# A message-passing kernel: 23 slots of 128 edges whose node features VectorE copies column by column in SBUF, in place of POOL's gathers

## The chip, the core and the metric

The kernel runs on one core of a Trainium2 chip. Its engines are PE (TensorE, matrix products), DVE (VectorE), ACT (ScalarE), POOL (GpSimd) and SP (SyncE, which only issues transfers here); each runs its own queue of instructions in order, and semaphores tie them together. SBUF is the on-chip memory, PSUM holds what PE writes. The metric is the device time of one execution in microseconds (us), the median of several runs; one more execution is taken with the hardware profiler.

## The reference

A graph has 12,500 nodes with 64 features (`x`) and 200,000 edges, sorted by their target `dst`. For each edge the features of its source and its target node go through a small network, the 64 edge features through another, and the product of both, scaled by a cutoff of the distance, is added up at the target node:

```python
nodes = node_state[edges].reshape(num_edges, -1)          # x[src], x[dst]
gates = ssp(edge_state @ We1 + be1) @ We2 + be2
gates = gates * (1.0 - sigmoid(5.0 * (edges_distance - (CUTOFF - 1.5))))
h = ssp(nodes @ Wn1 + bn1) @ Wn2 + bn2
message_sum = zeros_like(node_state).at[edges[:, 1]].add(h * gates)
new_state = node_state + (ssp(message_sum @ Ws1 + bs1) @ Ws2 + bs2)
return layernorm(x + new_state)
```

`ssp` is softplus less log 2. All is float32.

## The kernel before

**Steps and slots.** The edges are worked off in `NG` = 391 steps of 512 edges. A step has K = 4 slots of 128 edges, one edge to a partition. `src` is random, so the source features of a slot are fetched row by row; `dst` is sorted, so the targets of 256 edges lie within a window of 42 nodes, and the kernel reads that window's part of a table (x times the lower half of Wn1, made in the preparation) as a piece of a weight matrix `wns`.

**How the source rows come in.** For most slots POOL issues one indirect transfer each (`gather`, L231), which fetches 128 rows of 64 values into `xg[:, k, :64]`; tile `xg` has AHEAD + BEHIND = 19 buffers, and the program asks for step i + 14 in step i. A gather has to wait until its buffer's old tile is no longer read, that is, for the scatter product of the step 19 earlier. 47 of the 1,564 slots (`slots_by_rows`) are instead fetched by 128 single-row transfers, 7 in each step from SP's queue and 9 from ACT's (`fetch`, L257), and DVE copies the comparison's columns next to them (L296).

**One step i of the main loop**, in the order in which it is written; every engine takes its part in that order (`manual_schedule`):

- SP: loads for step i + 5 (edge features `eT`, L278; table pieces into `wns`, L286), then 7 row fetches. POOL: the gathers of step i + 14.
- PE: four transposes of step i + 1 (`tx`, L307), which turn edges x features into features x edges. ACT copies the result to SBUF (`xT`, L314).
- PE: bias products (L319, L354); the scatter product of step i - 2 (L383), which adds up messages by the comparison's ones and zeros; the edge product (L324); the node product `wns` x `xT` (L330), two halves h of 256 edges, of slots k = h and k = 2 + h. ACT takes exponential and logarithm of the result (L341, L344).
- DVE: `window` adds the scatter product to `sums` at two positions that are known only at run time (L400; the positions are loaded into DVE's registers by L391). PE: second layer of step i (L361 and L366, from `s`). DVE: two products with the cutoff (`hcut` L375, `message` L379), then softplus of step i + 1 (L349, writes `s`), then `onehot` of step i + 3: a comparison of the edges' targets with 0 to 41 (L293, writes `xg[:, :, 64:106]`).
- Parts of finished blocks of 512 nodes (`node_block`) are spread over the steps, some before `onehot`, some behind it.

**Preparation.** 56 gathers are issued at the start. PE makes the table in 14 pieces (L591), ACT and DVE copy each to SBUF (L593, L594, tile `tb`), SP stores it (L595), and DVE clears `sums` behind it (L596). In between, behind the fourth piece, DVE prepares positions and biases (L598 to L605), and behind the sixth `rel` (L609, L612).

**Registers.** A position known at run time is read from SBUF by the engine's own sequencer (`values_load_multi_w_load_instructions`, a TENSOR_LOAD in the trace), and a FUSED_REGOPS works out the address ahead of each instruction that uses it.

Of the kernel before, what the change touches and what calls it, by code (L numbers as in the profile page):

```python
# [42 lines left out]
F32 = mybir.dt.float32  # L43
# [35 lines left out]
READY = (5, 7)  # L79
LANDED = 4  # L80
CUTOFF = 5.0
EPS = 1e-5
# [22 lines left out]
def slots_by_rows(NG):  # L105

    slots = []
    for queue in range(2):
        n = 0
        for g in range(READY[queue], NG - 2):  # L110
            if (g - READY[queue] - ROWS_FROM + 1) * ROWS[queue] >= (n + 1) * P:
                slots.append((queue, g, K - 1 - queue))
                n += 1
    return slots


# [7 lines left out]
def gnn_resnorm_kernel(ctx: ExitStack, tc: tile.TileContext, a: dict, out: bass.AP, E: int):  # L124
# [58 lines left out]
    row3 = const.tile([PIECES, 2, K, D], BF16, name="row3")  # L183
    rs3 = const.tile([PIECES, K, D], BF16, name="rs3")
    wns = const.tile([DW, REST, 2, 2 * D], F32, name="wns")

# [34 lines left out]
    def gather(g):  # L221
# [3 lines left out]
        for k in range(K):  # L225
            if (g, k) in by_rows:
                continue
            if padding(g, k):
                nc.vector.memset(xg[:, k, :D], 0.0)
                continue  # L230
            note(("gather", g), nc.gpsimd.indirect_dma_start(  # L231
                out=xg[:, k, :D], out_offset=None, in_=x,
                in_offset=bass.IndirectOffsetOnAxis(ap=src_i[:, g, k : k + 1], axis=0)))
# [39 lines left out]
    def load(g):  # L273
# [11 lines left out]
        for h in range(2):  # L285
            behind(note(("load", g), nc.sync.dma_start(  # L286
                wns[D:DW, g % REST, h, :].bitcast(U8),
                table_bytes[:, bass.ds(bases[g][h], 8 * D * W)].rearrange("o (w f) -> (o w) f", w=W))), old)

    xTs, zs, us, ss, ghs, hs, msgs, scs = ({} for _ in range(8))  # L290

# [35 lines left out]
    def layer1_node(g):  # L327
        for h in range(2):
            zn = zs[g][:, h, HE * (1 - h) : HE * (2 - h)]
            nc.tensor.matmul(zn, wns[:, g % REST, h, :], xTs[g][:, h], start=True, stop=True,  # L330
                             skip_group_check=True)

    def z_of(g):
# [156 lines left out]
    with tc.manual_schedule():  # L490
# [4 lines left out]
        with tc.tile_pool(name="prep", bufs=1) as prep:  # L495
# [11 lines left out]
            for i in range(3):  # L507
                load_x(i)
            nc.sync.dma_start(rows_i, a["rows"])
            dist = cut.rearrange("p g k -> p (g k)")  # L510
            nc.sync.dma_start(dist, a["dist_l"])
# [3 lines left out]
            for g in range(AHEAD):  # L515
# [13 lines left out]
            nc.scalar.dma_start(wns[:D].rearrange("f r h o -> f (r h) o"),  # L529
                                a["Wn1"][:D, :].rearrange("f (r o) -> f r o", r=1).to_broadcast([D, 2 * REST, 2 * D]))  # L530

            dst_f = dst_h.bitcast(F32)
# [53 lines left out]
            for i in range(PARTS):  # L586
# [10 lines left out]
                if i == 1:  # L597
                    nc.vector.tensor_copy(base_i[:1], base_b[:1])  # L598
                    nc.vector.tensor_scalar(base_i[32:33], base_b[32:33], float(8 * D), None, OP.mult)
                    nc.vector.tensor_scalar(rows_i, rows_i, float(4 * D), None, OP.mult)  # L600
                    for k in range(2):
                        nc.vector.tensor_copy(be3[:, k, :], rows[:, 0, :])
# [11 lines left out]

        with tc.tile_pool(name="finish", bufs=1) as finish:
            blocks = list(zip(node_blocks(N), block_steps(N, NG)))
            last = NG - 1
# [14 lines left out]
            for i in range(-1, last - 1):  # L632
                now = parts.pop(i, [])
                early = [part for part in now if part.tensor]
                at(load, i + LOADS)
                read_rows(i, 0, ROWS[0])
                fetch(i, 0, ROWS[0])
# [24 lines left out]
                for part in early:  # L662
                    part.others()
                at(onehot, i + 3)
                for part in now:
                    if not part.tensor:
# [133 lines left out]
def layouts(inputs):  # L800
# [22 lines left out]
    for queue, columns in enumerate(row_columns(NG)):  # L823
        chosen = [out["src_l"].reshape(P, NG, K)[:, g, k] for q, g, k in slots_by_rows(NG) if q == queue]
        v = padded(np.concatenate(chosen), P * columns, 0).reshape(-1, P, READ)
        rows.append(v.transpose(1, 0, 2).reshape(P, columns))
    out["rows"] = np.ascontiguousarray(np.concatenate(rows, axis=1))
    out["dst_l"] = lanes(dst, dst[-1])
    out["dist_l"] = lanes(dist, 1e6)
# [43 lines left out]
```

## Time and profile before

| | |
|---|---|
| runs | 2685.64 us median of 3 (2685.46 to 2688.31) |
| profiled execution | 2686.47 us; span 2684.7 us |
| granted TensorE clock | 0.815 on average |
| busy | PE 84%, PEld 65%, POOL 54%, DVE 39%, ACT 36% |
| gathers (L231) | 1,516, 951 ns each |
| DMA | 53 GB/s on average |

The profile is of one execution. In a line of the timeline the first number is the start in us from the span's start, the second the time it took; what stands in brackets is the idle time of the engine just before it and what ended that. In a group's line the numbers behind the count are the busy time, the mean of one in ns, and the idle time before the group's instructions with what ended most of it. PE and PEld are the products and the weight loads of TensorE; the ends of products are modelled. A releaser is inferred from semaphores, and "remote" and "issue" are what is left where none was found.

### The profile page before, as it was taken

The page shows a single profiled execution, that of the slowest core. Times are in us where ns is not written, and L with a number is a line of the kernel's source. Part 1 is how long each engine was busy: PE and PEld are TensorE (multiplying, and loading weights), DVE is VectorE, ACT ScalarE, POOL GpSimd, SP SyncE. Part 2 cuts the span into 40 slices and gives each one's busy share as a digit, 9 for nine tenths or more (in the row PEclk, how much of TensorE's full clock was granted, in tenths as well). Part 3 has the DMA queues.
Part 4 walks back from the last instruction along what each step waited for, and adds up shares of the span by engine and source line. Part 5 has one row for each costly group of instructions (what it writes and reads, how often), then busy time and mean ns, then how long its engine had stood idle before and what let it go on. Part 6 is the DMA issues. An engine that isn't in the chain of part 4 may idle for free.

```text
span 2684.7 us, 47845 instructions
## 1 busy us (share of the span) xinstructions
PE 2243.6 (84%) x11373; PEld 1754.9 (65%) x11373; DVE 1052.4 (39%) x2767; ACT 969.6 (36%) x1318; POOL 1441.8 (54%) x1520
## 2 busy tenths in 40 slices
PE   2489888988888888888889788888888888888897
PEld 1467666766666666666667666666666667666676
DVE  1233333333334333344333443434433443444445
ACT  0133333333333333333333333333334333333344
POOL 7335555555555555555555555555555555555520
PEclk9987788788788778788777888778878887787878
DMA  6222222222222212222222222222222222222210
GB/s 159 82 64 52 48 51 49 48 49 48 49 52 50 49 47 51 51 52 47 52 46 50 51 49 53 53 50 53 51 50 50 50 58 48 54 52 50 52 44 25
DMA packets 150911, 143.53 MB, mean 53 GB/s; under 512 B 51887, under 2 KB 98395, under 8 KB 150626
## 3 DMA queue, kind: packets, MB, share of 16 engines
q1 hardware_dynamic: 94090, 88.26, 11.6%
q0 software_dynamic: 48512, 49.77, 9.5%
q10 hardware_dynamic: 8024, 2.37, 0.4%
q8 instruction: 97, 1.59, 0.2%
q14 instruction: 188, 1.54, 0.2%
HBM read 130.59 MB, written 9.63 MB: 52 GB/s over the span
## 4 chain that ended last, share of the span: by engine, by line
PE 64%; another core or an unknown queue 11%; ACTq 10%; ACT 7%; issue 5%; DVE 1%; DMA 0%; DVEq 0%; SPq 0%
PE z L330 16%; PE gh L366 12%; PE z L383 10%; ACTq L257 10%; PE gh L361 7%; PE tx L307 6%; ACT xT L314 6%; PE z L324 4%; PE gh L354 3%; PE z L319 2%; PE tx L419 1%; PE z L591 1%; ACTq L245 1%; PE tx L450 1%
## 5 line engine op out<-in xcount | busy, mean ns | idle before, releaser
L231 POOL DMA_INDIRECT xg<-in_x,src_i x1516 | 1441.6, 951 | 1144.8 <-PE z L383 353.1
L330 PE MATMUL z<-xT,wns 106*128 106x256 f32 x1564 | 574.1, 503 | 322.9 <-ACT xT L314 309.5
L330 PEld LDWEIGHTS z<-xT,wns 106*128 106x128 f32 x1564 | 361.3, 246 | 486.6 <-ACT xT L314 407.9
L341 ACT ACTIVATE u<-z 128x768 f32<-128x768 f32 x392 | 317.4, 810 | 830.4 <-issue 362.4
L366 PE MATMUL gh<-consts,s 128*128 128x64 f32 x3128 | 493.1, 313 | 0.0
L400 DVE TENSOR_TENSOR sums<-sums,z 64x42 f32 x778 | 153.0, 197 | 863.4 <-issue 626.8
L366 PEld LDWEIGHTS gh<-consts,s 128*128 128x128 f32 x3128 | 490.2, 238 | 0.1
L314 ACT COPY xT<-tx 106x512 f32<-106x512 f32 x391 | 228.9, 586 | 670.9 <-remote 231.5
L375 DVE TENSOR_TENSOR h<-gh,cut 128x256 f32<-128x256 f32 x391 | 166.1, 425 | 618.2 <-PE z L383 239.7
L344 ACT ACTIVATE u<-u,one 128x768 f32<-128x768 f32 x392 | 365.9, 934 | 69.7 <-issue 53.3
L349 DVE SCALAR_TENSOR_TENSOR s<-u,z 128x768 f32<-128x768 f32 x392 | 369.4, 943 | 11.1 <-ACT u L344 9.8
L361 PEld LDWEIGHTS gh<-consts,s 128*128 128x128 f32 x1564 | 304.0, 247 | 70.1 <-DVE s L349 32.8
L383 PEld LDWEIGHTS z<-xg,msg 128*128 128x128 f32 x1556 | 240.3, 221 | 152.8 <-issue 148.5
L361 PE MATMUL gh<-consts,s 128*128 128x128 f32 x1564 | 313.8, 335 | 1.8 <-DVE s L349 1.8
L383 PE MATMUL z<-xg,msg 128*128 128x84 f32 x1556 | 306.2, 327 | 0.9 <-DVE msg L379 0.2
L324 PE MATMUL z<-eT,consts 128*128 128x256 f32 x782 | 295.4, 465 | 0.0
L307 PE MATMUL tx<-consts,xg 128*106 128x128 f32 x1517 | 278.6, 312 | 6.4 <-DMA wns<-table 6.4
L307 PEld LDWEIGHTS tx<-consts,xg 128*106 128x106 f32 x1517 | 216.0, 169 | 10.6 <-issue 8.0
L379 DVE TENSOR_TENSOR msg<-gh,h 128x256 f32<-128x256 f32 x391 | 166.0, 425 | 13.4
L354 PE MATMUL gh<-row,ones 3*128 3x512 bf16 x391 | 170.0, 435 | 0.0
L324 PEld LDWEIGHTS z<-eT,consts 128*128 128x128 f32 x782 | 141.7, 226 | 1.2 <-issue 1.2
L293 DVE TENSOR_TENSOR xg<-consts,rel 128x168 f32<-128x168 f32 x391 | 129.9, 332 | 0.0
(93 smaller groups left out, 609.5 us busy)
## 6 DMA issues: line engine op xcount, KB each, us to landing
xr<-in_x ACTq DMA_DIRECT2D x3328, 0.2 KB
eT<-in_eT SPq DMA_DIRECT2D x195, 256.0 KB
xr<-in_x SPq DMA_DIRECT2D x2688, 0.2 KB
xg<-in_x,src_i POOLq DMA_INDIRECT x1516
wns<-table SPq DMA_DIRECT2D x782, 21.0 KB
table<-tb SPq DMA_DIRECT2D x14, 448.0 KB
sums<-in_xT SPq DMA_DIRECT2D x7, 455.0 KB
y<-in_x SPq DMA_DIRECT2D x24, 128.0 KB
```

The costliest lines, as they stand in the source:

```text
L231: note(("gather", g), nc.gpsimd.indirect_dma_start(out=xg[:, k, :D], out_offset=None, in_=x, in_offset=bass.IndirectOffsetOnAxis(ap=src_i[ ...
L257: ins = queues[queue].dma_start(row_tiles[n, "in"][r : r + 1, :D].bitcast(U8), x_bytes[:, bass.ds(row_at[queue].pop(0), 4 * D)])
L307: ins = nc.tensor.transpose(tx[:, k, :], xgs[g][:, k, :DW], ident)
L314: note(("xcopy", g), nc.scalar.copy(xT, xTs[g]))
L324: nc.tensor.matmul(zs[g][:, 0, :HE], we1.rearrange("a h d -> a (h d)"), eTs[g], start=False, stop=True, skip_group_check=True)
L330: nc.tensor.matmul(zn, wns[:, g % REST, h, :], xTs[g][:, h], start=True, stop=True, skip_group_check=True)
L341: nc.scalar.activation(us[g][:, part], z_of(g)[:, part], AF.Exp)
L344: nc.scalar.activation(us[g][:, part], us[g][:, part], AF.Ln, bias=one)
L349: nc.vector.scalar_tensor_tensor(ss[g].rearrange("p i t e -> p (i t e)")[:, part], us[g][:, part], BIG, z_of(g)[:, part], OP.min, OP.max)
L361: nc.tensor.matmul(v[:, 0, t], ss[g][:, 0, t, :], we2, start=False, stop=False, skip_group_check=True)
L366: nc.tensor.matmul(ghs[g][:, 1, 2 * t + h, :], ss[g][:, 1 + h, t, :], wn2, start=False, stop=h == 1 and t == 1, skip_group_check=True)
L383: ins = nc.tensor.matmul(sc, msgs[g][:, 2 * t : 2 * t + 2, :].rearrange("p h f -> p (h f)"), xgs[g][:, 2 * t : 2 * t + 2, D:DW], start=t = ...
```

## The change

For 23 slots (k = 1 of steps 26, 42, ... 378; `slots_by_columns`), POOL no longer gathers. A transposed copy `xh` of x lies in SBUF: 128 partitions x 6,250, nodes 0 to 6,249 in the upper 64 partitions and nodes 6,250 to 12,499 in the lower 64. From step 8 on DVE, behind `onehot`, loads eight column numbers into registers and copies eight columns of `xh`, one for each of eight edges, into a tile `column` of 128 x 128; after 16 steps the tile is full. One DVE instruction then keeps, for each edge, the half of the partitions that holds its node (`sides` against `border`) and writes `chosen`. In the step's node product PE adds `wn1_twice` x `chosen` for that slot. In `xg` the slot's 64 columns are set to zero by DVE, so the transposes and the product with `wns` stay as they were and add only the target's part. `xh` is loaded in four parts from SP's queue in steps 0 to 3; column numbers, sides and the doubled weights are loaded and converted in the preparation.

```diff
@@ -78,6 +78,9 @@
 ROWS_FROM = -1
 READY = (5, 7)
 LANDED = 4
+COLUMNS = 8
+COLUMNS_FROM = 8
+XH_PARTS = 4
 CUTOFF = 5.0
 EPS = 1e-5
 LN2 = 0.6931471805599453
@@ -112,6 +115,20 @@
                 slots.append((queue, g, K - 1 - queue))
                 n += 1
     return slots
+
+
+def slots_by_columns(NG):
+
+    slots = []
+    for g in range(NG - 2):
+        if (g - 3 - COLUMNS_FROM + 1) * COLUMNS >= (len(slots) + 1) * P:
+            slots.append((g, 1))
+    return slots
+
+
+def column_columns(NG):
+
+    return -(-len(slots_by_columns(NG)) // COLUMNS) * COLUMNS
 
 
 def row_columns(NG):
@@ -182,6 +199,14 @@
     be3 = const.tile([PIECES, 2, D], BF16, name="be3")
     row3 = const.tile([PIECES, 2, K, D], BF16, name="row3")
     rs3 = const.tile([PIECES, K, D], BF16, name="rs3")
+    half_n = a["xh"].shape[1]
+    by_columns = {slot: n for n, slot in enumerate(slots_by_columns(NG))}
+    columns_i = const.tile([P, column_columns(NG)], I32, name="columns_i")
+    sides_i = const.tile([P, len(by_columns) * P], I32, name="sides_i")
+    sides = sides_i.bitcast(F32)
+    sign = const.tile([P, 1], F32, name="sign")
+    border = const.tile([P, 1], F32, name="border")
+    wn1_twice = const.tile([P, 2 * D], F32, name="wn1_twice")
     wns = const.tile([DW, REST, 2, 2 * D], F32, name="wns")
 
     xgs, xrs, eTs = {}, {}, {}
@@ -225,7 +250,7 @@
         for k in range(K):
             if (g, k) in by_rows:
                 continue
-            if padding(g, k):
+            if padding(g, k) or (g, k) in by_columns:
                 nc.vector.memset(xg[:, k, :D], 0.0)
                 continue
             note(("gather", g), nc.gpsimd.indirect_dma_start(
@@ -287,6 +312,28 @@
                 wns[D:DW, g % REST, h, :].bitcast(U8),
                 table_bytes[:, bass.ds(bases[g][h], 8 * D * W)].rearrange("o (w f) -> (o w) f", w=W))), old)
 
+    column_tiles, chosen_columns, columns_done = {}, {}, [0]
+
+    def columns(i, pool):
+
+        n = columns_done[0]
+        if i < COLUMNS_FROM or n >= len(by_columns) * P:
+            return
+        p, q = (n // COLUMNS) % P, n // (COLUMNS * P) * COLUMNS
+        _, at = nc.values_load_multi_w_load_instructions(
+            columns_i[p : p + 1, q : q + COLUMNS], engines=[DVE], min_val=0, max_val=half_n - 1,
+            skip_runtime_bounds_check_because="src holds rows of x")
+        slot = list(by_columns)[n // P]
+        if n % P == 0:
+            column_tiles[slot] = pool.tile([P, P], F32, name="column", bufs=1)
+        for j in range(COLUMNS):
+            nc.vector.tensor_copy(column_tiles[slot][:, n % P + j : n % P + j + 1], xh[:, bass.ds(at[j], 1)])
+        columns_done[0] += COLUMNS
+        if columns_done[0] % P == 0:
+            chosen_columns[slot] = pool.tile([P, P], F32, name="chosen", bufs=1)
+            nc.vector.scalar_tensor_tensor(chosen_columns[slot], sides[:, n // P * P : (n // P + 1) * P], border,
+                                           column_tiles[slot], OP.is_ge, OP.mult)
+
     xTs, zs, us, ss, ghs, hs, msgs, scs = ({} for _ in range(8))
 
     def onehot(g):
@@ -327,8 +374,12 @@
     def layer1_node(g):
         for h in range(2):
             zn = zs[g][:, h, HE * (1 - h) : HE * (2 - h)]
-            nc.tensor.matmul(zn, wns[:, g % REST, h, :], xTs[g][:, h], start=True, stop=True,
+            chosen = [t for t in range(2) if (g, 2 * t + h) in by_columns]
+            nc.tensor.matmul(zn, wns[:, g % REST, h, :], xTs[g][:, h], start=True, stop=not chosen,
                              skip_group_check=True)
+            for t in chosen:
+                nc.tensor.matmul(zn[:, t * P : (t + 1) * P], wn1_twice, chosen_columns[g, 2 * t + h], start=False,
+                                 stop=True, skip_group_check=True)
 
     def z_of(g):
         return zs[g].rearrange("p b e -> p (b e)")[:, : 3 * HE]
@@ -507,6 +558,8 @@
             for i in range(3):
                 load_x(i)
             nc.sync.dma_start(rows_i, a["rows"])
+            nc.sync.dma_start(columns_i, a["columns"])
+            nc.sync.dma_start(sides_i, a["sides"].partition_broadcast(P))
             dist = cut.rearrange("p g k -> p (g k)")
             nc.sync.dma_start(dist, a["dist_l"])
             dst_i = rel.bitcast(I32)
@@ -528,6 +581,11 @@
             nc.scalar.dma_start(consts[:, FIRST:], a["consts"][:, FIRST:])
             nc.scalar.dma_start(wns[:D].rearrange("f r h o -> f (r h) o"),
                                 a["Wn1"][:D, :].rearrange("f (r o) -> f r o", r=1).to_broadcast([D, 2 * REST, 2 * D]))
+
+            for h in range(2):
+                nc.scalar.dma_start(wn1_twice[h * D : (h + 1) * D, :], a["Wn1"][:D, :])
+                nc.vector.memset(sign[h * D : (h + 1) * D], 2.0 * h - 1.0)
+                nc.vector.memset(border[h * D : (h + 1) * D], float(half_n if h else 1 - half_n))
 
             dst_f = dst_h.bitcast(F32)
             nc.vector.tensor_copy(dst_f, dst_h)
@@ -598,6 +656,10 @@
                     nc.vector.tensor_copy(base_i[:1], base_b[:1])
                     nc.vector.tensor_scalar(base_i[32:33], base_b[32:33], float(8 * D), None, OP.mult)
                     nc.vector.tensor_scalar(rows_i, rows_i, float(4 * D), None, OP.mult)
+                    upper = prep.tile([P, column_columns(NG)], F32, name="upper")
+                    nc.vector.tensor_scalar(upper, columns_i, float(half_n), float(-half_n), OP.is_ge, OP.mult)
+                    nc.vector.tensor_tensor(columns_i, columns_i, upper, OP.add)
+                    nc.vector.tensor_scalar(sides, sides_i, sign, None, OP.mult)
                     for k in range(2):
                         nc.vector.tensor_copy(be3[:, k, :], rows[:, 0, :])
                     for k in range(K):
@@ -613,6 +675,7 @@
 
 
         with tc.tile_pool(name="finish", bufs=1) as finish:
+            xh = finish.tile([P, half_n], F32, name="xh")
             blocks = list(zip(node_blocks(N), block_steps(N, NG)))
             last = NG - 1
             parts, begun, complete, rest = {}, None, 0, []
@@ -633,6 +696,9 @@
                 now = parts.pop(i, [])
                 early = [part for part in now if part.tensor]
                 at(load, i + LOADS)
+                if 0 <= i < XH_PARTS:
+                    part = slice(half_n * i // XH_PARTS, half_n * (i + 1) // XH_PARTS)
+                    nc.sync.dma_start(xh[:, part], a["xh"][:, part])
                 read_rows(i, 0, ROWS[0])
                 fetch(i, 0, ROWS[0])
                 if i >= 0:
@@ -662,6 +728,7 @@
                 for part in early:
                     part.others()
                 at(onehot, i + 3)
+                columns(i, finish)
                 for part in now:
                     if not part.tensor:
                         part.others()
@@ -825,6 +892,12 @@
         v = padded(np.concatenate(chosen), P * columns, 0).reshape(-1, P, READ)
         rows.append(v.transpose(1, 0, 2).reshape(P, columns))
     out["rows"] = np.ascontiguousarray(np.concatenate(rows, axis=1))
+    chosen = np.concatenate([out["src_l"].reshape(P, NG, K)[:, g, k] for g, k in slots_by_columns(NG)])
+    out["sides"] = np.ascontiguousarray(chosen)
+    v = padded(chosen, P * column_columns(NG), 0).reshape(-1, P, COLUMNS)
+    out["columns"] = np.ascontiguousarray(v.transpose(1, 0, 2).reshape(P, -1))
+    half_n = -(-N // 2)
+    out["xh"] = np.ascontiguousarray(np.concatenate([x[:half_n].T, padded(x[half_n:], half_n, 0.0).T]))
     out["dst_l"] = lanes(dst, dst[-1])
     out["dist_l"] = lanes(dist, 1e6)
     out["dst_h"] = np.ascontiguousarray(padded(dst, NR * P * HE, dst[-1]).reshape(NR, P, HE).transpose(1, 0, 2))
```

## The prediction

> **What bounds the kernel now.** First the page: busy shares and the costliest groups.
>
> ```profile
> PE 2243.6 (84%) x11373; PEld 1754.9 (65%) x11373; DVE 1052.4 (39%) x2767; ACT 969.6 (36%) x1318; POOL 1441.8 (54%) x1520
> ...
> L231 POOL DMA_INDIRECT xg<-in_x,src_i x1516 | 1441.6, 951 | 1144.8 <-PE z L383 353.1 <-issue 352.1 <-DVE s L349 182.5
> ```
>
> PE looks like the bound, POOL like an engine with half its time free. So I asked next for the busy time in two stretches of 71 us: one in which POOL has no gathers left, and one in the middle.
>
> ```profile
> 2589.00:2660.00 71.00, 68.98 (x446) 56.93 (x446) 42.61 (x118) 36.60 (x55) 0.00 (x0) 0.97 0.11 31
> 1480.00:1551.00 71.00, 58.58 (x309) 46.20 (x309) 28.25 (x76) 27.15 (x38) 40.22 (x44) 0.83 0.22 52
> ```
>
> The columns are PE, PEld, DVE, ACT and POOL busy, granted clock, DMA share, GB/s. Without gathers PE is 97% busy at a clock of 0.97, and a step (from one xT copy, L314, to the next) takes 4.58 us on average over the last 14. With them PE is 83% busy. What PE waits for stands in the timeline of POOL and that of ACT, around a step that issues three gathers:
>
> ```profile
> 1553.31 0.95 POOL L231 DMA_INDIRECT xg<-in_x,src_i  x1 [1.50 <-DVE s L349]
> 1554.56 0.95 POOL L231 DMA_INDIRECT xg<-in_x,src_i  x1 [0.30 <-issue]
> 1555.82 0.95 POOL L231 DMA_INDIRECT xg<-in_x,src_i  x1 [0.30 <-issue]
> 1558.25 0.94 POOL L231 DMA_INDIRECT xg<-in_x,src_i  x1 [1.48 <-PE z L383]
> 1559.49 0.95 POOL L231 DMA_INDIRECT xg<-in_x,src_i  x1 [0.30 <-issue]
> 1560.75 0.95 POOL L231 DMA_INDIRECT xg<-in_x,src_i  x1 [0.30 <-issue]
> 1562.00 0.95 POOL L231 DMA_INDIRECT xg<-in_x,src_i  x1 [0.30 <-issue]
> ```
>
> ```profile
> 1553.00 0.59 ACT L314 COPY xT<-tx 106x512 f32<-106x512 f32 x1 [1.65 <-PE z L383]
> ...
> 1557.94 0.59 ACT L314 COPY xT<-tx 106x512 f32<-106x512 f32 x1 [0.94 <-PE z L383]
> ...
> 1564.27 0.59 ACT L314 COPY xT<-tx 106x512 f32<-106x512 f32 x1 [2.37 <-remote]
> ```
>
> The xT copy starts 2.12 us after the start of the last gather of its batch (1555.82 to 1557.94), and again 2.27 us after (1562.00 to 1564.27); 0.31 us later POOL starts the next batch, which waits for the scatter of the same step (a tile has 19 buffers, and POOL has used them all). Over steps 20 to 369 that distance is 1.9 to 2.6 us in 92% of them, while the distance from the end of the transposes, for which the copy waits, runs from 0.04 to 3 us. So PE's finished work is told to the others only when the batch of gathers is through; why, the trace does not show. A step is then three issue intervals of 1.25 us, 2.2 us and 0.31 us: 6.26 us, and with one gather fewer 5.01. Medians: 6.37 for 302 steps with four, 5.12 for 41 with three.
>
> **Part by part.** Base: the profiled execution took 2686.47 us (span 2684.7 and 1.8 around it), 0.83 above the median of 2685.64.
>
> *Removed: 23 gathers.* They are 16 steps apart (g = 26, 42, ... 378). The 41 steps with three gathers price one, since the kernel already fetches 47 slots in another way. Not all of 1.25 us stays: after such a step PE may be late. A step with three and the next, which has four, take 12.55 us together, two with four 13.29: 0.74 saved. Over three steps it is 18.84 against 19.99 (1.15, standard error 0.22), over five 32.16 against 33.39 (1.24, 0.20). I take 1.0: 23 x 1.0 = -23 us; ends 0.74 and 1.25, -17 and -29. POOL's queue loses only these; the zeroing of xg's 64 columns instead is a DVE memset (L229: 112 ns), whose waits are for gathers of 19 tiles ago.
>
> *Added on DVE in 368 steps:* one load of eight registers and eight copies, each with a register operation. The load is like L391's (median 528 ns; it runs in DVE's queue, ahead of the engine). A copy of 128x1 is not in the trace: small copies follow each other by 0.09 to 0.10 us (L602 to L605, 110.03 to 110.87), the two dynamic additions of `window` by 0.20, held to the end of the first. So eight take 0.8 to 1.6 us. What is queued behind them is the next `window`, whose own load (0.53) and register operation (0.09) no longer run early: 1.42 us at least, 2.8 if the first load is bare too. The cover:
>
> ```profile
> 1506.42 0.94 DVE L349 SCALAR_TENSOR_TENSOR s<-u,z 128x768 f32<-128x768 f32 x1
> 1507.28 0.33 DVE L293 TENSOR_TENSOR xg<-consts,rel 128x168 f32<-128x168 f32 x1
> 1510.04 0.41 DVE L400 TENSOR_TENSOR sums<-sums,z 64x42 f32 x2 [2.43 <-issue]
> 1510.50 0.42 DVE L375 TENSOR_TENSOR h<-gh,cut 128x256 f32<-128x256 f32 x1
> ```
>
> The copies go between L293 and L400, an idle stretch of 2.23 us on average. Then L375 waits another 1.64 for PE, and from the end of L349 to L361, which reads s, there are 1.50. Taking these three from 1.42 and from 2.8 us step by step, L375 is late by 6.6 and 61 us in sum, L361 by 0 and 7. PE is reached last, so: +1 us, ends 0 and 7.
>
> *Added on PE:* 23 matmuls of 128x128 f32 in `layer1_node`; transposes and the old product stay. L361 has the shape: 335 ns a record, two records, 0.11 us apart at full clock, so 0.22 to 0.27 us: 6 us if all count. In 85% of steps PE's work is over 0.3 us or more ahead of its signal, and that cover hides them: +2, ends 0 and 6. The 23 selections (128x128, two inputs, like L569's 272 ns) go into the same DVE idle stretch.
>
> *Preparation.* DVE multiplies `sides`, 128x2944, int32 to f32. L609 (128x1564) took 0.90 us, so about 1.7; with two small ones (L600: 0.19 each) 2.1. At L612's rate (0.97 us for 782) it would be 4. They sit between the fourth and fifth copy to `tb` (107.28 and 110.95), and PE's run L591 x112 from 111.55 to 135.84, without a gap, starts on the fifth: +2.1, on the path. The three small transfers and the 1.5 MB broadcast of `sides` are issued early on SP's and ACT's queues, ahead of dist, dst and four parts of xT on SP's; all of these are wanted after 106 us, behind the stream of 56 gathers (to 99.5 us). If they slow that stream, 0 to 2: +0.5. The four parts of `xh` (0.8 MB each) go out in steps 0 to 3 on SP's queue, behind loads for five steps later and ahead of the row fetches of the step; the stores to the table showed 448 KB every 3 us, so each part takes up to 5.4 us beside gathers. Signals 1 us late in four steps give +4: I take +1.
>
> Sum: -23 + 1 + 2 + 2.1 + 0.5 + 1 = -16.4, so 2686.5 - 16.4 = 2670.
>
> **A rule against the change.** Does a copy from SBUF to SBUF hold a gather? Row: a gather that starts while a copy runs,
>
> ```profile
> 2181.45 0.95 POOL L231 DMA_INDIRECT xg<-in_x,src_i  x1 [3.11 <-PE z L383]
> 2181.45 0.22 DVE L296 COPY xr<-xg 128x42 f32<-128x42 f32 x1
> ```
>
> and one that starts 0.04 us behind the start of L293, an operation with two inputs in SBUF:
>
> ```profile
> 353.47 1.11 POOL L231 DMA_INDIRECT xg<-in_x,src_i  x1 [2.69 <-PE z L383]
> ```
>
> The five gathers with L296 running at their start took 946 ns each, those just behind L293 up to 1.11 us. So I set the copies at nothing. The Trainium skill (SBUF — State Buffer, Who interferes with whom) says otherwise: an fp32 copy within SBUF can run in a two-port mode that takes the port pair shared with GpSimd, and the later of the two blocks until the other ends. By it eight copies of 0.1 us would hold POOL 0.8 us in each of 368 steps, of which 85% count: +250 us, 2920. The trace's copies are wider than one element and only 47, so it does not settle the case fully.
>
> **Rivals.** (1) *The copies hold the gathers:* slower. For it: L293 does it, and copies now run at the first and second gather of nearly every step. Against it: the rows above. Price: 0.155 us (1.107 less 0.952) on one gather a step, x 368 x 0.85 = 48 us, so 2718; half of it 2694. It decides from 16.4 / (368 x 0.85) = 0.05 us a step, a mean gather above about 965 ns. (2) *PE takes the gain back:* the clock is granted at 0.8 between 0.5 and 1.0, and steps just behind a three-gather step are often over 7 us. At 0.3 us a gather, -7 + 6.6 = 0: 2686. (3) *DVE is late:* 3.8 us instead of 1.42 to 2.8 puts L361 30 us late in sum: 2699.
>
> **Chances.** Forecast 0.62 (2657 to 2681; of that 0.02 within 0.2%), rival 2 0.14 (same 0.10, faster 0.02, slower 0.02), rivals 1 and 3 together 0.24 (slower 0.23, same 0.01). 0.2%, 5.4 us, is about what a measurement of this kernel can tell from no change. That gives faster 0.64, same 0.13, slower 0.23. The unknowns reach from 2686.5 - 29 + 2 = 2660 to 2686.5 - 17 + 23 = 2692; taking in half of rivals 1 and 3 on top and a little below: 2656 to 2700.
>
> **What would show it.** Right: 1493 gathers with a mean near 951 ns; xT copies still 2.2 us behind the last gather; 23 more steps near 5.1 us; POOL still idle about 1.5 us a step; L400's wait shorter, L361's waits for s still small; PE's long L591 run from about 114. Wrong: gathers above 965 ns on average (rival 1), step sums around the new short steps not shorter (rival 2), PE waiting for s by tens of us (rival 3).

## The result, and the profile after

Over 20 runs of each kernel the changed one takes 2694.31 us (median) and the one before 2682.32: a ratio of 1.0048, 95% interval 1.0027 to 1.0069. The change makes this kernel slower, by 12 us where 16 less were forecast. The profiled execution took 2700.15 us (span 2698.2, granted clock 0.807; before 2686.47, 2684.7, 0.815).

In the page after, the busy shares and four groups answer to those shown of before (line numbers are those of the changed kernel: gather L256, `hcut` L426, `window` L451, column copies L330):

```profile
PE 2275.5 (84%) x11419; PEld 1778.3 (66%) x11419; DVE 1283.1 (48%) x5764; ACT 969.1 (36%) x1318; POOL 1415.2 (52%) x1497
...
L256 POOL DMA_INDIRECT xg<-in_x,src_i x1493 | 1415.0, 948 | 1188.0 <-PE z L434 387.4
...
L426 DVE TENSOR_TENSOR h<-gh,cut 128x256 f32<-128x256 f32 x391 | 165.8, 424 | 760.3 <-PE tx L354 242.1
...
L451 DVE TENSOR_TENSOR sums<-sums,z 64x42 f32 x778 | 152.9, 197 | 470.6 <-issue 330.8
...
L330 DVE COPY column<-xh 128x1 f32 x2944 | 244.2, 144 | 35.4 <-issue 34.6
```

The 23 gathers are gone, and the others are no longer than they were (948 ns, before 951), so the copies do not hold POOL. POOL waits for PE's scatter product longer nevertheless (387.4 us, before 353.1). DVE's wait ahead of `window` is shorter, as was meant (470.6, before 863.4 at its L400), but its wait ahead of `hcut`, for PE, is 142 us longer (760.3, before 618.2 at its L375). In the stretches of 71 us, the middle of the kernel and the end without gathers:

```profile
1480.00:1551.00 71.00, 63.80 (x314) 48.99 (x314) 35.33 (x162) 26.77 (x38) 39.27 (x42) 0.78 0.21 51
2600.00:2671.00 71.00, 66.44 (x430) 54.99 (x429) 45.33 (x144) 36.76 (x55) 2.66 (x3) 0.98 0.13 37
```

At the end, where all but three gathers are through, little has changed: clock 0.98, and the last 14 steps take 4.60 us on average (before 4.58). In the middle PE works off about as many products (314, before 309) in more busy time, at a clock of 0.78. The loss lies in the steps that gather: steps 20 to 369 take 6.562 us on average, before 6.531, although 59 of them have fewer than four gathers, before 44. A step with four takes 6.772 us (before 6.679).

What has grown is the last piece of a step, from the start of the batch's last gather to the next xT copy; I call it the *tail*. The prediction took it as fixed at 2.2 us. Over steps 20 to 369 of the two traces it takes 2.31 us on average, before 2.20, which is 39 us in sum. (The way from an xT copy to the first gather takes 8 us more in sum, that from the first gather to the last 37 less.) PE being late is not what makes most of it. In the steps in which the transposes, for which the xT copy waits, had ended over 0.3 us before it (by their modelled ends), the tail is 2.25 us (305 steps), before 2.15 (297), which makes some 29 of the 39 us. I call these steps *held*.

A second thing is new in the timeline of DVE, set against ACT's xT copy. Before the change:

```profile
1510.04 0.41 DVE L400 TENSOR_TENSOR sums<-sums,z 64x42 f32 x2 [2.43 <-issue]
1510.50 0.42 DVE L375 TENSOR_TENSOR h<-gh,cut 128x256 f32<-128x256 f32 x1
1510.95 0.42 DVE L379 TENSOR_TENSOR msg<-gh,h 128x256 f32<-128x256 f32 x1
1511.42 0.95 DVE L349 SCALAR_TENSOR_TENSOR s<-u,z 128x768 f32<-128x768 f32 x1
```

```profile
1513.60 0.59 ACT L314 COPY xT<-tx 106x512 f32<-106x512 f32 x1 [2.21 <-PE z L383]
```

`hcut` starts 3.1 us ahead of the next xT copy, and the softplus that PE needs for its next second layer is ready 1.2 us ahead of it. After the change:

```profile
1512.63 0.42 DVE L426 TENSOR_TENSOR h<-gh,cut 128x256 f32<-128x256 f32 x1 [2.31 <-PE z L434]
1513.09 0.42 DVE L430 TENSOR_TENSOR msg<-gh,h 128x256 f32<-128x256 f32 x1
1513.43 0.94 DVE L400 SCALAR_TENSOR_TENSOR s<-u,z 128x768 f32<-128x768 f32 x1
```

```profile
1512.74 0.59 ACT L361 COPY xT<-tx 106x512 f32<-106x512 f32 x1 [1.73 <-remote]
```

Here `hcut` waits until the moment in which the xT copy too is released, behind the batch of gathers, and softplus is ready only 1.6 us into the next step. The prediction knew that the xT copy is told of PE's work only when the batch is through. It had not seen that the second layer's signal was told in the middle of the batch in 57% of these 350 steps before the change (`hcut` over 0.25 us ahead of the xT copy). After it, that is so in 19%. I call such a step *ahead*; the expectations below call it softplus ahead. But the steps that are not ahead are not the dear ones: after the change the tail takes 2.25 us in the steps that are not ahead and 2.57 in those that are, before it 2.22 and 2.19.

### The profile page after: what moved, and what is told of

Read it like the earlier page. It is cut to its first block, busy times and chain, and to the rows that moved or that the text cites. A ratio compares the mean times of both kernels' runs of the same rounds, so it can differ in the third digit from the quotient of the medians.

```text
span 2698.2 us, 53942 instructions
## 1 busy us (share of the span) xinstructions
PE 2275.5 (84%) x11419; PEld 1778.3 (66%) x11419; DVE 1283.1 (48%) x5764; ACT 969.1 (36%) x1318; POOL 1415.2 (52%) x1497
## 4 chain that ended last, share of the span: by engine, by line
PE 63%; ACTq 11%; another core or an unknown queue 11%; ACT 7%; issue 5%; DVE 1%; DMA 1%; DVEq 0%; SPq 0%
PE z L378 15%; PE gh L417 13%; ACTq L282 10%; PE z L434 9%; PE gh L412 7%; PE tx L354 7%; ACT xT L361 5%; PE z L371 4%; PE gh L405 3%; PE z L366 2%; PE tx L470 1%; PE z L649 1%; ACTq L270 1%; PE tx L501 1%
## 5 line engine op out<-in xcount | busy, mean ns | idle before, releaser
L256 POOL DMA_INDIRECT xg<-in_x,src_i x1493 | 1415.0, 948 | 1188.0 <-PE z L434 387.4
L378 PE MATMUL z<-xT,wns 106*128 106x256 f32 x1564 | 562.4, 495 | 297.3 <-ACT xT L361 289.6
L426 DVE TENSOR_TENSOR h<-gh,cut 128x256 f32<-128x256 f32 x391 | 165.8, 424 | 760.3 <-PE tx L354 242.1
L417 PE MATMUL gh<-consts,s 128*128 128x64 f32 x3128 | 506.7, 319 | 0.0
L417 PEld LDWEIGHTS gh<-consts,s 128*128 128x128 f32 x3128 | 504.5, 244 | 0.0
L451 DVE TENSOR_TENSOR sums<-sums,z 64x42 f32 x778 | 152.9, 197 | 470.6 <-issue 330.8
L400 DVE SCALAR_TENSOR_TENSOR s<-u,z 128x768 f32<-128x768 f32 x392 | 368.7, 941 | 10.9 <-ACT u L395 9.9
L412 PEld LDWEIGHTS gh<-consts,s 128*128 128x128 f32 x1564 | 297.9, 247 | 85.5 <-DVE s L400 45.2
L412 PE MATMUL gh<-consts,s 128*128 128x128 f32 x1564 | 322.8, 341 | 4.6 <-issue 2.8
L330 DVE COPY column<-xh 128x1 f32 x2944 | 244.2, 144 | 35.4 <-issue 34.6
L354 PEld LDWEIGHTS tx<-consts,xg 128*106 128x106 f32 x1517 | 221.4, 172 | 10.9 <-issue 8.3
```

What stands on the lines that cost most here:

```text
L256: note(("gather", g), nc.gpsimd.indirect_dma_start(out=xg[:, k, :D], out_offset=None, in_=x, in_offset=bass.IndirectOffsetOnAxis(ap=src_i[ ...
L354: ins = nc.tensor.transpose(tx[:, k, :], xgs[g][:, k, :DW], ident)
L400: nc.vector.scalar_tensor_tensor(ss[g].rearrange("p i t e -> p (i t e)")[:, part], us[g][:, part], BIG, z_of(g)[:, part], OP.min, OP.max)
L412: nc.tensor.matmul(v[:, 0, t], ss[g][:, 0, t, :], we2, start=False, stop=False, skip_group_check=True)
L417: nc.tensor.matmul(ghs[g][:, 1, 2 * t + h, :], ss[g][:, 1 + h, t, :], wn2, start=False, stop=h == 1 and t == 1, skip_group_check=True)
```

## The experiments

The runs met the kernel before at two levels: 2634 to 2683 us with a mean granted clock of 0.81 to 0.84 (the low level, that of the result), and 1937 to 1941 us with 0.97 (the high level). The level belongs to the set of runs, not to the kernel: chip 14 showed 1937 in one set and 2640 in another. Every ratio below is to the kernel before on the same chip in the same set; brackets hold the 95% interval. A ratio need not be the quotient of the two medians beside it.

### The parts, at the high level

Four kernels. *No copies*: the changed kernel without its register load and copies (the 23 slots lack their source nodes).

```diff
-        _, at = nc.values_load_multi_w_load_instructions(...)
...
-        for j in range(COLUMNS):
-            nc.vector.tensor_copy(column_tiles[slot][:, ...], xh[:, bass.ds(at[j], 1)])
+            nc.vector.memset(column_tiles[slot], 0.0)
```

> The changed kernel without DVE's register loads and column copies (the column tile is set to zero once for a slot, so the source part of those 23 slots is left out of the result). Against the kernel before, in ratio. Theory A, the loads and copies on DVE are what costs (they keep PE's layer-2 signal behind the batch of gathers and the xT copy 0.07 us later in each step): the gathers' gain shows, 10 to 16 us faster than before, ratio 0.994 to 0.996, and the distance from the last gather's start to the xT copy is back at 2.20 us (2.26 in the changed kernel). Theory B, a gather less is worth nothing because PE's clock or its backlog takes it back: it stays 5 to 10 us slower than before, ratio 1.002 to 1.004, distance at 2.26 or not.

*No gathers*: the kernel before, with the 23 gathers replaced by zeroing.

```diff
-            if padding(g, k):
+            if padding(g, k) or (g >= 26 and (g - 26) % 16 == 0 and g < 379 and k == 1):
```

> The kernel before, with the 23 slots' gathers replaced by the DVE memset alone: no xh, no preparation, no copies, no product (the source part of 23 slots is left out of the result). The gain by itself. Theory A: 17 to 27 us faster, ratio 0.990 to 0.994, with 23 more steps of three gathers. Theory B: within 5 us of before, ratio 0.998 to 1.002.

*Copies only*: the changed kernel with all its gathers; copies, loads and `xh` stay, the product with `chosen` goes.

```diff
-            if padding(g, k) or (g, k) in by_columns:
+            if padding(g, k):
...
+            chosen = []
```

> The changed kernel with all 23 gathers kept on POOL and without the product of wn1_twice and chosen; loads, copies and selections are done and not used. The cost by itself. Theory A: the sum of the cost of about 30 us, ratio 1.010 to 1.013, of which 8 us stand before step 20. Theory B: it costs what the changed kernel lost, 12 us, ratio 1.004.

*Fixed columns*: the changed kernel with copies from columns that are fixed when the program is built, without register load and address operations.

```diff
-            nc.vector.tensor_copy(column_tiles[slot][:, ...], xh[:, bass.ds(at[j], 1)])
+            nc.vector.tensor_copy(column_tiles[slot][:, ...], xh[:, (n * 37 + j * 797) % half_n :][:, :1])
```

> The changed kernel with the same eight copies at positions fixed in the program: no register load, no address arithmetic (the columns are not those of the edges). If the copies cost, as in the changed kernel: ratio 1.004. If the register load or the address operations cost: near the kernel without copies, 0.995 by theory A.

The four came at the high level: no copies 0.9863 [0.9847, 0.9879], no gathers 0.9861 [0.9846, 0.9876], copies only 1.0007 [0.9997, 1.0016], fixed columns 0.9882 [0.9867, 0.9897]. Three of them were repeated in the hope of the low level, with a fourth meant to hold the loads alone:

> The kernel without loads and copies again (the source part of 23 slots is left out), for a chip whose clock is granted at 0.81, where the changed kernel took 2699 us and the kernel before 2682. Theory C1, on such a chip the copies on DVE are the cost: 12 to 20 us faster than before, ratio 0.993 to 0.996, and the distance from the last gather's start to the xT copy is 2.20 us again. Theory C2, on such a chip a gather less is worth nothing and what costs is in the preparation and the start: ratio 1.001 to 1.005, distance 2.25. If the chip grants 0.97 again, 0.986 by both.

> The kernel before with 23 gathers left out and nothing else (their source part is left out of the result), for the chip at 0.81. C1: 17 to 27 us faster, ratio 0.990 to 0.994. C2: ratio 0.998 to 1.002.

> All gathers kept, loads, copies, selections, xh and preparation added, for the chip at 0.81. C1: 25 to 40 us slower than before, ratio 1.009 to 1.015, distance 2.26. C2: 10 to 17 us slower, ratio 1.004 to 1.006.

> The changed kernel with the eight-register load of each step kept and the copies and their address operations left out (the source part of 23 slots is left out). C1 with the copies at fault: as the kernel without loads and copies, 0.993 to 0.996. C1 with the load at fault: as the changed kernel, 1.004 to 1.006. On a chip at 0.97: 0.986 to 0.987.

High level again: 0.9861 [0.9846, 0.9876], 0.9851 [0.9836, 0.9867], 1.0016 [1.0006, 1.0025], and 0.9868 [0.9853, 0.9883] for the fourth. At this level a removed gather is worth 1.2 us (0.0139 to 0.0149 of 1938 us over 23), and all that the change adds costs at most a few us. By that the change should be a clear gain, so the loss had to come with the level.

### The change itself, at both levels

> The changed kernel itself once more. On the chip of the runs without copies, without gathers and with copies alone, the kernel before took 1937 us at a clock of 0.97, not 2682 us at 0.81, and 23 gathers less were worth 27 us there. Theory C, the change's worth depends on whether PE's clock is throttled: at a clock of 0.97 it gains 20 to 27 us, ratio 0.986 to 0.990; at 0.81 it loses as in the result, ratio 1.003 to 1.007. Theory B (a gather less is worth nothing on any chip): 1.00 or above in both.

> The changed kernel itself, beside the kernel before on the same chip. Its ratio depends on the chip's clock. On a chip that grants 0.97 (before near 1937 us) the parts add up to 0.986 for the gathers, +0.001 for the copies and +0.002 for the register loads: about 0.988, so 1914 us, and a ratio over 0.993 would say that the parts don't add. On a chip that grants 0.81 (before near 2682 us) 1.005, as in the result.

> The changed kernel itself, beside the kernel before on the same chip. At the low clock 1.005 to 1.007, softplus ahead in 20 to 25% of the steps. At a clock of 0.97, where it has not run yet, the parts add up to 0.988 (23 gathers 0.986, fixed copies +0.001, register loads and address operations not known, at most +0.002): there the change would be faster by over 1%, and the sign of its effect would follow the clock.

Low level, chip 5: 1.0056 [1.002, 1.0091]. Low level, chip 14: 2662.06 us against 2639.95, 1.0069 [1.0033, 1.0105]. High level, chip 4: 1913.73 us against 1940.73, **0.9872** [0.9857, 0.9888]. The same program loses 0.5 to 0.7% at the one level and gains 1.3% at the other, where 89% of its steps are ahead.

What differs between the levels, apart from the clock, is seen in SP's queue too. The timelines of SP show the seven row fetches of one step, as one group; before the change at the low level, the changed kernel there (chip 14), and the changed kernel at the high level:

```profile
1510.59 3.80 SPq L257 DMA_DIRECT2D xr<-in_x  x7
```

```profile
1508.56 4.81 SPq L282 DMA_DIRECT2D xr<-in_x  x7
```

```profile
1101.29 2.19 SPq L282 DMA_DIRECT2D xr<-in_x  x7
```

At the low level SP's register moves between them, 29 ns otherwise, are stretched: in the trace of before 395 of 2,458 take over 0.1 us, the longest 1.4; in that of the changed kernel at the high level none takes over 0.04. I count a stall where SP's next instruction, with nothing to wait for, begins over 0.1 us after the start of a move (0.45 after that of an issue). By this count nearly every low-level step with four gathers has stalls, and the last of them ends 0.14 to 0.19 us ahead of the xT copy (medians of the traces); at the high level 3 of 4 such steps have none. That the two end together suggests that one thing keeps back both SP's queue and PE's signals, the *hold* from here on; it is argued from this, not shown. The stalls sum to 2.77 us a step before and 2.96 to 3.05 in the three traces of the changed kernel at the low level; without copies, of which more below, to 2.62 and 2.83. (On chip 14 alone: 2.62 without copies, 2.96 with them.) How early the first stall comes depends too much on what is counted to read anything from it.

### No copies, at the low level

> The changed kernel without its register loads and column copies (the column tile is set to zero, so the 23 slots lack their source nodes). On a chip that grants 0.97: 0.986 once more. On a chip that grants 0.81 two theories differ. C1, DVE's copies and loads undo the gain there: without them the 23 gathers show, -17 to -29 us less some 5 us of preparation, ratio 0.990 to 0.995. C2, on such a chip a removed gather is worth nothing, because something other than POOL's batch sets the step (TensorE's clock): ratio 1.000 to 1.006, as with the copies.

The same chip and set as the 1.0069: 2619.31 us, **0.9916** [0.9883, 0.9949]. C1 is right and C2 is not: at the low level too the change without copies gains 21 us, and copies with their loads cost 43 us (2662.06 less 2619.31; 40 by the ratios). The tail shows where most of it goes. A last gather and the xT copy behind it, first no copies, then the changed kernel:

```profile
1487.39 0.94 POOL L256 DMA_INDIRECT xg<-in_x,src_i  x1 [0.30 <-issue]
1489.45 0.59 ACT L357 COPY xT<-tx 106x512 f32<-106x512 f32 x1 [1.78 <-PE z L430]
```

```profile
1516.39 0.95 POOL L256 DMA_INDIRECT xg<-in_x,src_i  x1 [0.30 <-issue]
1518.57 0.59 ACT L361 COPY xT<-tx 106x512 f32<-106x512 f32 x1 [2.26 <-PE z L434]
```

These tails take 2.06 and 2.18 us. In the held steps of the two traces the mean is 2.050 us (281 steps) and 2.143 (280), with standard errors of 0.017 and 0.011: 0.09 us more with copies, 26 us over 280 steps, of the 32 us between the two profiled executions (2638.47 and 2670.35). In held steps that lie wholly at full clock it is 2.022 and 2.135. So PE's signal comes later behind the batch, in steps in which PE itself was done before and at full clock too. Each trace is one execution; what speaks for the reading is that the traces of before and after differ by the same 0.09 us (their chips are not on record).

The wait of PE for softplus grows too:

```profile
PEld gh L408 <- DVE s L396: 23.2, 63, 2.0
```

```profile
PEld gh L412 <- DVE s L400: 49.1, 138, 2.0
```

The columns are the wait in us, how often, and the longest. 71% of the steps are ahead without copies, 24% with them. The 26 us between the two waits are not a price to be added up, though: by the pages of the two runs PE is idle for 449 us in all without copies (2636.7 less 2188.1) and for 429 with them (2668.4 less 2239.6). One comparison speaks against PE being merely later here. Of the steps with four gathers that follow one that was not ahead, take those in which the second layer's last product ended 2.5 to 3.0 us after the batch's first gather: its signal came in the middle of the batch in 47 of 64 before the change and 27 of 39 without copies, but in 13 of 84, 8 of 95 and 13 of 84 in the three traces of the changed kernel. With the product at the same moment, the signal comes later.

### Copies or loads

> The changed kernel with its load of eight registers in each step, but without the column copies (the tile is set to zero, so the 23 slots lack their source nodes). Where the clock is granted at about 0.82: D1, the loss comes with the register loads, which now run in the middle of a batch of gathers: ratio 1.000 to 1.007, DVE's softplus starts behind the next xT copy in about 80% of the steps, as in the changed kernel. D2, it comes with the eight copies: ratio 0.989 to 0.994, softplus ahead of the next xT copy in over 55% of the steps, as in the kernel without both. Where the clock is granted at 0.97: 0.987 by both.

> The changed kernel with its eight copies in each step from columns that are fixed when the program is built (so the 23 slots get other nodes than theirs), without the load of registers. Where the clock is granted at about 0.82: D1 (the register loads): ratio 0.989 to 0.995, softplus ahead of the next xT copy in over 50% of the steps. D2 (the copies): 1.000 to 1.007, softplus behind it in about 80%. Where the clock is granted at 0.97: 0.988 by both.

High level once more, 0.9866 and 0.9869: nothing told apart. Then *bases first*, a change of order alone:

```diff
+                for g in behind_by(i + 1):
+                    window_bases(g)
                 columns(i, finish)
```

> The changed kernel with one order changed: the load of the two positions for the next step's window stands ahead of the load of the eight column numbers and of the copies, so that it runs early again, as before the change, and no register load runs between two gathers' signals in the middle of a batch. Where the clock is granted at about 0.82: D1' (the late load of the window's positions is what costs): ratio 0.988 to 0.996, softplus ahead of the next xT copy in over 45% of the steps. D2 (the copies) or D1'' (the load of eight registers itself, wherever it stands): 1.000 to 1.007, softplus ahead in 20 to 25%. Where the clock is granted at 0.97: 0.987 to 0.989, with softplus ahead in all steps.

Low level: 1.0069 [1.0039, 1.0098], 27% of the steps ahead. The window's load ran early again (it ended 0.6 us after the batch's first gather in the median, in the changed kernel 2.4), but the loss stayed: my guess D1' fell.

> The changed kernel with its load of eight registers in each step, but without the column copies (the tile is set to zero, so the 23 slots lack their source nodes), hoped for at the low clock. There: D1'', the load of registers lengthens the hold, ratio 1.000 to 1.007, softplus ahead of the next xT copy in 20 to 30% of the steps; D2, the copies do, ratio 0.989 to 0.995, softplus ahead in over 50%. In between, 0.995 to 1.000 with 30 to 50%, would say that both have a share. At a clock of 0.97: 0.987 by both, as before.

Low level: 0.9901 [0.9868, 0.9934], 59% ahead. This says nothing for D2, though: the trace has 392 register loads on DVE, as many as before, where the changed kernel has 760. The unused loads had been left out of the program, here and in the two earlier runs of that name, so it is the kernel without copies again, on another chip.

> The changed kernel with its eight copies in each step from columns that are fixed when the program is built (so the 23 slots get other nodes than theirs), without load of registers and without address operations. The run called loads_only held no loads after all (its trace has one register load a step, as before), so copies and loads are still not told apart at the low clock. There: if the copies lengthen the hold, ratio 1.000 to 1.007 and softplus ahead of the next xT copy in 20 to 30% of the steps; if the loads or the address operations do, 0.989 to 0.995 and over 50%; a share of both, 0.995 to 1.000. At a clock of 0.97: 0.988 once more.

Low level, the chip of bases first: 1.0015 [0.9983, 1.0046], 41% ahead. The copies alone take back about 1.1% (from 0.990 to 0.992), some 28 us. That leaves some 0.5%, 14 us, to loads and address operations; the interval of this run and that of bases first, on the same chip, overlap by a little, so this second part is less sure. The low-level traces in order of the ratio:

| kernel | ratio | steps ahead | PE waits for softplus, us |
|---|---|---|---|
| no copies (two chips) | 0.9901, 0.9916 | 59%, 71% | 28.1, 23.2 |
| before | 1 | 57% | 32.8 |
| fixed columns | 1.0015 | 41% | 37.4 |
| changed (three traces) | 1.0048 to 1.0069 | 19 to 24% | 45.2 to 51.1 |
| bases first | 1.0069 | 27% | 44.3 |

The tail of held steps is 2.111 us with fixed columns and 2.143 with bases first, both on chip 8. It differs as much from chip to chip (without copies 2.050 on chip 14, 2.143 on the chip of the low-level run meant to hold the loads alone), so I compare it on one chip alone.

### One wide copy

```diff
-        _, at = nc.values_load_multi_w_load_instructions(...)
...
-        for j in range(COLUMNS):
-            nc.vector.tensor_copy(column_tiles[slot][:, ...], xh[:, bass.ds(at[j], 1)])
+            nc.vector.memset(column_tiles[slot], 0.0)
+        nc.vector.tensor_copy(xh[:, 5400:6200], xh[:, n : n + 800])
```

> The changed kernel with one copy of 128x800 within SBUF in each step instead of the eight copies and their register load (so the 23 slots lack their source nodes); I estimate 0.5 to 0.9 us for it, from the conversions of 128x1564 (0.90 us) and 128x782 (0.97 us). At the low clock: if it is DVE's busy time between the comparison and the next window that lengthens the hold, ratio 1.000 to 1.007 and softplus ahead of the next xT copy in 20 to 40% of the steps, like the eight fixed copies (1.0015, 41%); if it is the number of DVE's instructions, 0.988 to 0.994 and over 55%, like the kernel without copies (0.991, 71%). At a clock of 0.97 neither shows: 0.986 to 0.990.

High level: 1.007 [1.0056, 1.0084], beside 0.9872 for the change on the same chip. I had expected nothing at that level. A group and a gather of this kernel, the copy that the gather met, and the same group of the changed kernel on that chip:

```profile
L256 POOL DMA_INDIRECT xg<-in_x,src_i x1493 | 1456.5, 976 | 458.7 <-issue 334.8 <-DMA xg<-in_x,src_i 45.6 <-PE z L375 14.0
```

```profile
1102.22 1.21 POOL L256 DMA_INDIRECT xg<-in_x,src_i  x1 [0.30 <-PE z L431]
```

```profile
1102.04 0.57 DVE L327 COPY xh<-xh 128x800 f32<-128x800 f32 x1
```

```profile
L256 POOL DMA_INDIRECT xg<-in_x,src_i x1493 | 1422.5, 953 | 458.5 <-issue 342.7
```

This gather began 0.18 us into the copy and took 1.21 us instead of 0.95. The 40 gathers that began with 0.4 to 0.5 us of a wide copy left took 1.27 us on average; those with under 0.1 us left, 0.945. Over all gathers it is 23 ns x 1493 = 34 us, of 39 us between the two kernels. Beside the copies of 128x1 the gathers that began inside a group of them took 0.946 us however much was left of it. Whether DVE's time or its number of instructions lengthens the hold was not settled, since this run missed the low level.

## Why the prediction was wrong

**The step that failed** is "+1 us, ends 0 and 7" for the work on DVE. At the low level copies with their loads cost 40 to 43 us. The work itself was priced too high, if anything: a group of eight copies takes 0.57 us in the median (61 ns from one to the next), 0.96 or less in nine of ten, where 0.8 to 1.6 us were taken. The cover was wrong. I took DVE's idle stretch ahead of `window` and its wait for PE ahead of `hcut` as free time, and asked only how far the copies push `hcut` past the moment at which it ran in the trace. PE's signals and the tail of 2.2 us behind the last gather stood fixed in that sum, and the forecast's own sign was "xT copies still 2.2 us behind the last gather". They were not fixed: with copies the tail of a held step is 0.09 us longer, which no single step would show and which makes 26 of the 32 us between the two traces of chip 14. The path that I priced, softplus late for PE, did show 12 us more waiting (45.2, before 32.8), but PE's idle time in all did not grow.

The measured 2694 lies inside the stated 2656 to 2700 by luck, since the upper part of that range was there for rivals whose mechanisms did not occur. The parts of the chances, by the way, add up to 0.62 for faster and 0.25 for slower, not to the 0.64 and 0.23 written there.

**The gathers**, -23 us: within their ends. Without copies the change gains 21 and 25 us at the low level, where the sum without the DVE term is 17.4; at the high level no gathers gains 27 to 29 us, at the end of 29. Gathers left out alone were not run at the low level.

**PE's product, preparation, xh**: small, as taken, as far as runs show it. At the high level no copies, which has all of these, and no gathers, which has none, differ by 0.0002 and 0.001, 0.4 and 2 us, each within its interval of some 3 us. The conversion of `sides` took 1.75 us and the two small ones 0.35, the forecast 2.1. In the profiled pair the first 20 steps are 5.0 us longer, but in the other two traces of the changed kernel 3 us shorter than in that of before; that is scatter.

**Rival 1** (the copies hold the gathers) is refuted for copies of 128x1: 948 ns, where 965 was the mark. The Trainium skill's rule (SBUF — State Buffer, Who interferes with whom) was weighed rightly for this change, since no gather met a hold; for a wide copy it holds, as the last experiment shows: the gather ends later by what was left of the copy, less some 0.1 us. The row that I set against it, copies of 128x42 taking 0.22 us, could not have shown it: what is left of so short a copy costs a gather next to nothing in the wide case too (0.966 us with 0.1 to 0.2 left). **Rival 2** (the clock takes the gain back): the kernel without copies keeps its gain at the same level, so a removed gather does not bring this on by itself. The clock is lower with copies, 0.823 against 0.841 on average over the runs on chip 14, and among the runs of one kernel, there and in the result, the time falls with the clock by some 10 to 16 us for each 0.01; so, if the clock came first, it could account for 18 to 28 of the 43 us. The longer tail speaks against that for the most part, since it is there in held steps at full clock too; for the rest, which of the two follows the other is open. **Rival 3** (DVE is late) named a wait that did grow, PE's for softplus, by 12 us of the 30 that it gave; its mechanism, copies that take 3.8 us, was not there, and that its 2699 comes near the result is luck.

**Left open:** why the copies lengthen the hold, by their time, their number or their address operations; what the hold is; and why there are two levels. The traces show only that SP's stalls end just ahead of PE's late signals, that both end with the batch of gathers, and that such stalls are rare at the high level, where the tail is 0.46 us (mean, steps with four gathers) instead of 2.2. Nor did I find a version that beats both kernels at both levels: bases first was the attempt.

## What to carry to other kernels

An idle stretch that ends on another engine's signal is cover only if the work put under it leaves that signal where it was. Write down which distances the sum takes as fixed, and measure their means over all steps after the change: here 0.09 us more in a distance of 2.2, in some 300 steps, comes to as much as 23 gathers gave. Price a change as a removed and an added part, and run each alone; here the removed part was right to a few us and the added one wrong by some forty. And measure at the clock at which the kernel will run: this change is worth -1.3% at one level and +0.5% at the other.

## What the hardware showed that I had not expected

- The same program at 1937 or 2640 us on one chip, with mean clocks of 0.97 and 0.83. In the traces the clock is granted either in full or by half: by half for 39% of the time of steps 20 to 369 in the kernel before at the low level, for 4% of it in the changed kernel at the high one. At the high level POOL issues gathers every 1.25 us nearly without a break, and PE is 93% busy.
- At the low level SP's register moves of 29 ns stretch to as much as 1.4 us while a batch of gathers runs, and PE's signals come late in the same stretch.
- A copy of 128x800 f32 within SBUF (0.57 us) lengthens a gather that starts under it by up to 0.4 us; eight copies of 128x1 in the same 0.57 us do not.
